# Two chunks of one image mixed in a later stage, and a finish with larger pieces, in a two-layer convolution and attention kernel

## The chip, the cores and the metric

The kernel runs on one core of one Trainium2 chip. The metric is device time in microseconds of one execution, as a median over runs. PE is TensorE (matmuls), DVE is VectorE, ACT is ScalarE, POOL is GpSimd, SP is SyncE, which issues most of the DMAs.

## The reference

Four images of 256 channels and 48 x 48 pixels go through two layers, each on a group-normalized input and each added to its input. Layer 0 is a 3 x 3 convolution and attention with 8 heads over the 2304 pixels. Layer 1 is a set of dynamic filters, mixed and normalized over all images:

```python
def _L1_conv_ref(x, W_cat, W_scale, gamma, beta):
    guidance = _conv(x, W_cat, pad=1)                  # 45 = 5 x 9 maps
    outs = [x]
    for i, d in enumerate((1, 6, 12, 24, 36)):
        w = softmax(guidance[:, 9 * i:9 * (i + 1)], axis=1)
        outs.append(_dyn_branch(x, w, d))              # 9 shifted copies, each times its map
    y = _conv(concatenate(outs, axis=1), W_scale, pad=0)   # 1536 -> 256 channels
    mean = jnp.mean(y, axis=(0, 2, 3)); var = jnp.var(y, axis=(0, 2, 3))
    return (y - mean) * rsqrt(var + EPS) * gamma + beta

x = x + _L0_conv_ref(_gn(x), ...)
x = x + _L1_conv_ref(_gn(x), ...)
```

## The kernel before, in words

The program is a fixed sequence: each engine executes its own list in order, and a list is in the order in which the Python code emits it. Semaphores join the lists. Channels lie on 128 partitions, in two halves (NH = 2). An image's rows are dealt to six chunks (NCK = 6) of 384 pixels (CH).

A loop over b runs through stages. Stage b holds the convolution and the q, k, v products of image b (`conv_qkv`: `pc` at L891, `pq` at L924, `pv` at L945) and, between their matmuls, the dynamic filters of image b-1; then attention of image b and its projection with group statistics follow. In a last stage (b == B, `alone`) image 3's filters run without a convolution beside them; then `finish` normalizes all four images and stores the result.

The filters of one image, chunk by chunk:

- guidance: `pg` (L1190) by matmuls over 45 rows in three pairs of chunks, transposed (`pt`), a softmax (`e`), transposed back (`pw`, L1244); the weights go to memory, `w_d` (L1251).
- near (dilation 1): SP loads each weight map spread over the partitions (`ws`, L1418), ACT copies it into a bank (`wb`, L1440), DVE multiplies it by the shifted image (`prod`, L1453), POOL adds it (`near`, L1458). `WBS` buffers hold loaded maps: 4, and 6 in the last stage.
- far (dilations 6 to 36): pixels are regrouped by transposes (`own`, `xa`, `xb`, L1307); weights come back by `wq` loads (L1279) and transposes `wT` (L1337) into masks (`bmat`, `amat`); matmuls (`far`, L1387) give results in banks, which `moved` (L1163 on ACT, L1165 on DVE) copies to one buffer `cat4`.
- mixes: 24 matmuls per chunk into `py` (L1536): the image itself (`gn`), four far sets, near. The result `y` is copied (L1493), its statistics are taken (L1499), and it is stored to `y_d`; image 3's stay on chip (`homes`).

`drive` decides at build time which of the streams (loads, far, near, filters, mixes) emits next. An account, `Clock`, adds up durations written in the code; a step yields the time at which it is due, and is emitted when PE's account has reached it; the convolution (`other`) fills the rest. In the last stage there is no `other`.

In the last stage `back()` loads y of images 0 and 1 and the residuals x1 of images 0, 1 and 2 (five loads of 2.36 MB on SP's queue, L1850 and L1851) when chunk 1's mixes begin; `last_loads` (from L1553) loads x1 of image 3 and y of image 2. Two groups of dummy matmuls `warm` (L970) stand at the stage's start. `finish` (from L1683) does, for images 0 and 1, 16 scalings of 576 elements on ACT and 16 sums on DVE, with one store each; for images 2 and 3, 24 scalings of 384, 12 sums of 768 and 8 stores.

Of the kernel before, what the change touches and what calls it, by code (L numbers as in the profile page):

```python
# [36 lines left out]
NEVER = float("inf")  # L37

# [17 lines left out]
def conv_preact_kernel(  # L56
# [36 lines left out]
    def rstd_of(dst, var):  # L93
        nc.vector.tensor_scalar(dst, var, EPS, None, ALU.add)
        nc.scalar.activation(dst, dst, AF.Sqrt)
        nc.vector.reciprocal(dst, dst)
# [443 lines left out]

    with tc.tile_pool(name="w", bufs=1) as wpool, tc.tile_pool(
# [93 lines left out]
        class Norm:  # L635
# [11 lines left out]
            def finish(self, psum_tile):  # L647

                mean = small.tile([P, NH], F32, tag=f"gmean{self.tag}", name=f"gmean_{self.name}", bufs=1)
                rstd = small.tile([P, NH], F32, tag=f"grstd{self.tag}", name=f"grstd_{self.name}", bufs=1)  # L650
                d2 = small.tile([P, NH], F32, tag="gd2", name=f"gd2_{self.name}")
                mv = self.mv
                for h in range(NH):
                    nc.vector.bn_aggr(mv[:, h, :], self.st[:, h].rearrange("p c s -> p (c s)"))
                yield
                pm = psum_tile(f"pm_{self.name}")
                nc.tensor.matmul(pm[:, :NH], gmat, mv[:, :, 0], start=True, stop=True)
                nc.scalar.copy(mean, pm[:, :NH])
                for h in range(NH):
                    nc.scalar.activation(  # L660
                        d2[:, h : h + 1], mv[:, h, 0:1], AF.Square, bias=mean[:, h : h + 1],
                        scale=-1.0,
                    )
                yield

                pv = psum_tile(f"pv_{self.name}")
                nc.tensor.matmul(pv[:, :NH], gmat, mv[:, :, 1], start=True, stop=False)
                nc.tensor.matmul(pv[:, :NH], gmat, d2, start=False, stop=True)
                rstd_of(rstd, pv[:, :NH])
                self.mean, self.rstd = mean, rstd  # L670
# [438 lines left out]
        def project(b, c, ao, pp, norm):  # L1109

            t = pads[b % 2]
            for o in range(NH):
                for g in range(NH):
                    nc.tensor.matmul(
                        pp[:, o, :CH],
                        wp[:, g, o * P : (o + 1) * P],
                        ao[:, g, c * CH : (c + 1) * CH],
                        start=(g == 0),
                        stop=(g == NH - 1),
                    )  # L1120
            for o in range(NH):
                x1 = inside(t, o, c * R, R)
                nc.vector.scalar_tensor_tensor(
                    out=x1, in0=rows_of(pp[:, o, :CH]), scalar=pbias[:, o : o + 1], in1=x1,
                    op0=ALU.add, op1=ALU.add,
                )
                norm.part(o, c, x1)
                nc.sync.dma_start(
                    out=rows_of(x1_d[b, :, o, c * CH : (c + 1) * CH]), in_=x1
                )  # L1130

        def dynamic_filters(b, ao, chunk, norm, other, pools):
# [27 lines left out]
            def moved(dst, src, size, *after):  # L1160

                if clock.t["ACT"] <= clock.t["DVE"]:
                    nc.scalar.copy(dst, src)  # L1163
                    return clock("ACT", 190 + 0.84 * size, *after)
                nc.vector.tensor_copy(dst, src)  # L1165
                return clock("DVE", 160 + 1.05 * size, *after)
# [12 lines left out]
            def weights(cs):  # L1179
# [61 lines left out]
                yield clock("DVE", 430) + 150  # L1241
# [44 lines left out]
            def far():  # L1286

                for c in range(NCK):
                    xT = work1.tile([P, PAIRS, C], F32, tag="xT", name=f"xT_{b}_{c}", bufs=1)

                    yield lambda: clock.t["DVE"] - 600
# [4 lines left out]
                    for h in range(NH):  # L1296
# [5 lines left out]
                            CH,  # L1302
                        )
# [38 lines left out]
                    end = clock("PE", 400)  # L1342
# [3 lines left out]
                    for t in range(3):  # L1346
# [7 lines left out]
                        end = clock("DVE", 460, end)  # L1354
                    free["k"].append(end)
                    rowsof = bmat.rearrange("p a (n y) x -> p (a n) y x", y=3)
                    for t in range(3):
                        yield lambda: clock.t["DVE"] - 600
# [9 lines left out]
                        end = clock("DVE", 960)  # L1368
                    cat = None
                    for p in range(PAIRS):  # L1370
# [25 lines left out]
                        clock("PE", 950)  # L1396
                        for s in range(2):
# [5 lines left out]
                                clock.t["PE"],  # L1403
# [7 lines left out]
            WBS, PRODS = 4 + 2 * alone, 2 + alone  # L1411
# [11 lines left out]
            def near():  # L1423

                for number, (c, k) in enumerate(sent):
                    centre = k == 4
                    if centre:
# [8 lines left out]
                        fetched[c, k][1], slot("wb", banks_w), clock.t["DVE"] - 600,  # L1436
# [71 lines left out]
            def mixes():  # L1508

                order = (0, *range(2, 2 + NF), 1)  # L1510
                for c in range(NCK):
                    now[0] = c
                    if alone and c == 1:
                        back()
                    for n in order:
# [34 lines left out]

            def last_loads():

                yield lambda: (  # L1553
                    0.0 if (NCK - 1, "own") in mixed and NCK - 1 in near_done
                    and len(far_ready) == NCK and (NCK - 2, "near") in mixed else NEVER
                )
                for o in range(NH):
                    nc.sync.dma_start(out=x1_3[:, o], in_=x1_d[B - 1, :, o])
                table(AF.Sqrt)
                for c in range(PRODS):  # L1560
                    t = work1.tile([P, NH, CH], F32, tag="prod", name=f"yp_{c}", bufs=PRODS)
                    y_2.append(t)
                    nc.sync.dma_start(out=t, in_=chunk_of(y_d, 2, c))
                yield lambda: 0.0 if (NCK - 1, "far") in mixed else NEVER
                t = work1.tile([P, NH, NF, CH], F32, tag="cat4", name="yc", bufs=1)
                t = t.rearrange("p h n c -> p (h n c)")
                for c in range(PRODS, NCK):
                    y_2.append(unit(t[:, NH * CH * (c - PRODS) : NH * CH * (c + 1 - PRODS)]))
                    nc.sync.dma_start(out=y_2[c], in_=chunk_of(y_d, 2, c))

            def drive(streams):

                due = [next(s, None) for s in streams]
                while any(d is not None for d in due):
# [9 lines left out]
                    else:  # L1584
                        got = next(other, None)
                        if got is None:
                            assert soonest < NEVER
                            clock.t["PE"] = soonest
                        else:
                            spent[0] += got  # L1590

            def warm(n):
                if alone:
                    busy(misc(f"warm_{b}_{n}"), n)
# [6 lines left out]
            warm(4)  # L1601
# [4 lines left out]
            warm(3)  # L1606
# [76 lines left out]
        def finish(work1):  # L1683

            ysc, ysh = batch_norm_of(yst, small, "f", ymv)

# [3 lines left out]
            def scaled(y, o):  # L1690
                nc.scalar.activation(
                    y, y, AF.Identity, bias=ysh[:, o : o + 1], scale=ysc[:, o : o + 1]
                )

            PART = 2 * STEP * WW
            for b, ty, tx in ((0, y_0, x1_0), (1, y_1, x1_1)):
                for o in range(NH):
                    for part in range(SIDE // 2):
                        y = ty[:, o].rearrange("p (c j w) -> p c j w", c=NCK, w=WW)
                        y = y[:, :, 2 * part : 2 * part + 2]  # L1700
                        scaled(y, o)
                        x1 = tx[:, o, part * PART : (part + 1) * PART]
                        both = x1.rearrange("p (j c w) -> p j c w", j=2, c=NCK)
                        nc.vector.tensor_tensor(
                            both, y.rearrange("p c j w -> p j c w"), both, ALU.add
                        )
                        nc.sync.dma_start(
                            out=image(b, o)[:, part * PART : (part + 1) * PART], in_=x1
                        )
            for b, ty, tx in ((2, y_2, x1_2), (3, homes, x1_3)):  # L1710
                for c in range(NCK):
                    for o in range(NH):
                        scaled(ty[c][:, o], o)
                    x1 = tx.rearrange("p h (j c w) -> p h j c w", c=NCK, w=WW)[:, :, :, c]
                    nc.vector.tensor_tensor(  # L1715
                        x1, ty[c].rearrange("p h (j w) -> p h j w", w=WW), x1, ALU.add
                    )
                for o in range(NH):
                    for cols in (slice(0, N // 2), slice(N // 2, N)):
                        nc.sync.dma_start(out=image(b, o)[:, cols], in_=tx[:, o, cols])  # L1720

        u_next = None
        norms = {}
        for b in range(B + 1):

            with tc.tile_pool(name=f"work1_{b}", bufs=2) as work1, tc.tile_pool(
                name=f"ps_c_{b}", bufs=2, space=PSUM
            ) as ps_c, tc.tile_pool(
                name=f"ps_w_{b}", bufs=2 if b == B else 1, space=PSUM
# [93 lines left out]
                else:  # L1823
                    if b == B:

                        y_0, x1_0, x1_2 = keep("q", "y_0"), keep("k", "x1_0"), keep("h", "x1_2")
                        y_1 = act.tile([P, NH, N], F32, tag="v", name="y_1")
                        x1_1, x1_3 = (t.rearrange("p h r w -> p h (r w)")[:, :, :N] for t in pads)

# [4 lines left out]
                        homes = []  # L1834
# [6 lines left out]
                        y_2 = []  # L1841
# [4 lines left out]
                        def back():  # L1846

                            for bb, ty, tx in ((0, y_0, x1_0), (1, y_1, x1_1), (2, None, x1_2)):
                                if ty is not None:
                                    nc.sync.dma_start(out=ty, in_=y_d[bb])  # L1850
                                nc.sync.dma_start(out=tx, in_=x1_d[bb])  # L1851
# [5 lines left out]
                    if b == B:  # L1857
                        finish(work1)
# [10 lines left out]
            load_pad(b)  # L1869
            scratch = upool.tile([P, NH, 3, C], F32, tag="u", name=f"scratch_{b}")  # L1870
# [100 lines left out]
```

## Time and profile before

| | us |
|---|---|
| median of 5 runs | 2794.53 (2792.67 to 2795.58) |
| profiled execution | 2793.88 |
| its span | 2792.0 |
| image 1 mixed, image 2's convolution | 1195 to 1492 |
| attention of image 2 | 1492 to 1868 |
| image 2 mixed, image 3's convolution | 1868 to 2163 |
| attention of image 3 | 2163 to 2534 |
| last stage: image 3's filters | 2534 to 2757 |
| finish | 2757 to 2792 |

The stages are cut at full microseconds: the first activation of the finish begins at 2753.75. In lines of the timeline the first number is the start in microseconds from the start of the span, the second the length, and a bracket at the end gives the idle time before it and what released it. In lines of windows each engine has its busy time and instruction count; PEclk is the granted TensorE clock, 1.00 being full.

### The profile page before, as it was taken

The numbers are of one execution on the slowest core, as the hardware profiler recorded it, in microseconds if no ns is written. First come the engines' busy times: TensorE is split into PE (matmuls) and PEld (weight loads), VectorE is DVE, ScalarE is ACT, GpSimd is POOL, SyncE is SP. The second block draws the span as 40 slices with busy tenths as digits, with TensorE's granted clock in tenths as the row PEclk, the third lists the DMA queues.
The fourth block names the chain that finished last, engine by engine and source line by source line (L and its number), as shares of the span: only waits on it lengthen the run. The fifth ranks groups of instructions, "written<-read, shape, count | busy, mean of one in ns | idle before, by whom it ended". The sixth has DMA issues, their size and how long they took to land. (4 is left out here: it accounts for less than half of the span.)

```text
span 2792.0 us, 42246 instructions
## 1 busy us (share of the span) xinstructions
PE 2651.8 (95%) x17122; PEld 1141.9 (41%) x17122; DVE 2023.7 (72%) x1948; ACT 1771.5 (63%) x2175; POOL 631.6 (23%) x583
## 2 busy tenths in 40 slices
PE   7999999899999999989999999989999999998983
PEld 5632223455652222445564222245566222234451
DVE  6578889566549888946646898875663989885665
ACT  3488988534359888833437898872334988873335
POOL 5100010535400110055510100134550000000452
PEclk9999999999999999999999999999999999999996
DMA  5514544232412544413350444522331244541545
GB/s 218 151 29 97 108 107 97 54 90 76 117 39 69 108 101 99 96 47 90 93 112 1 110 100 97 114 69 56 95 90 37 47 101 97 108 102 44 210 97 210
DMA packets 135946, 264.21 MB, mean 95 GB/s; under 512 B 65224, under 2 KB 100208, under 8 KB 134336
## 3 DMA queue, kind: packets, MB, share of 16 engines
q0 software_dynamic: 25952, 135.74, 21.1%
q1 hardware_dynamic: 109792, 125.70, 16.6%
q8 instruction: 136, 2.23, 0.3%
q14 instruction: 66, 0.54, 0.1%
HBM read 105.82 MB, written 32.89 MB: 50 GB/s over the span
## 5 line engine op out<-in xcount | busy, mean ns | idle before, releaser
L1044 DVE TENSOR_TENSOR acc<-acc,p 128x2048 f32<-128x2048 f32 (+1 forms) x572 | 1061.2, 1855 | 113.1 <-ACT p L1008 61.9
L1008 ACT ACTIVATE p<-se 128x1536 f32<-128x1536 f32 x648 | 938.6, 1448 | 0.0
L999 PE MATMUL so<-q,k 32*128 32x512 f32 (+1 forms) x1440 | 726.4, 592 | 14.1 <-ACT p L1007 13.6
L999 PE MATMUL se<-q,k 32*128 32x512 f32 (+1 forms) x4320 | 735.0, 592 | 0.0
L1028 PE MATMUL num<-p,vT 128*32 128x512 f32 (+1 forms) x5760 | 703.5, 560 | 4.6 <-ACT p L1008 2.4
L1007 ACT ACTIVATE p<-so 128x512 f32<-128x512 f32 x648 | 388.4, 599 | 184.1 <-PE se L999 74.7
L1458 POOL TENSOR_TENSOR near<-near,prod 128x768 f32<-128x768 f32 x192 | 348.2, 1814 | 401.3 <-DVE prod L1453 392.1
L999 PEld LDWEIGHTS so<-q,k 32*128 32x128 f32 x1440 | 216.1, 183 | 529.2 <-ACT p L1007 490.1
L1028 PEld LDWEIGHTS num<-p,vT 128*32 128x32 f32 x5760 | 132.9, 108 | 478.1 <-issue 444.3
L1048 POOL DMA_DIRECT2D scratch<-p x124 | 105.5, 851 | 770.2 <-ACT p L1008 566.0
L1536 PE MATMUL py<-far,wsc 128*128 128x384 f32 x768 | 256.8, 489 | 0.0
L1453 DVE TENSOR_TENSOR prod<-wb,pad 128x768 f32<-128x768 f32 x192 | 182.3, 955 | 99.1 <-ACT wb L1440 58.6
L1440 ACT COPY wb<-ws 128x384 f32<-128x384 f32 x216 | 107.9, 501 | 210.1 <-DVE prod L1453 194.9
L999 PEld LDWEIGHTS se<-q,k 32*128 32x128 f32 x4320 | 226.7, 183 | 5.4 <-ACT p L1008 4.1
L1536 PEld LDWEIGHTS py<-far,wsc 128*128 128x128 f32 x768 | 144.8, 191 | 100.1 <-issue 5.2
L1046 POOL DMA_DIRECT2D scratch<-p x32 | 17.9, 559 | 696.0 <-ACT p L1008 485.6
L1163 ACT COPY far<-far 128x512 f32<-128x512 f32 x82 | 87.9, 1099 | 127.2 <-PE far L1387 127.2
L891 PE MATMUL pc<-cv_q,u 128*128 128x288 f32 x576 | 155.1, 417 | 8.9 <-DVE cv_q L782 6.4
L1190 PE MATMUL pg<-pad,wcat 128*45 128x384 f32 x864 | 152.0, 497 | 6.5 <-DVE pad L631 4.0
L891 PE MATMUL pc<-cv_k,u 128*128 128x288 f32 x576 | 152.7, 410 | 1.6 <-ACT m L837 1.3
L891 PEld LDWEIGHTS pc<-cv_q,u 128*128 128x128 f32 x576 | 108.3, 193 | 47.2 <-DVE cv_q L782 6.5
L924 PE MATMUL pq<-hid,wqkv 128*128 128x384 f32 x384 | 125.3, 487 | 1.1 <-ACT q L931 0.6
(246 smaller groups left out, 2350.3 us busy)
## 6 DMA issues: line engine op xcount, KB each, us to landing
scratch<-p POOLq DMA_DIRECT2D x156, 768.0 KB, 5.7
ws<-w_d SPq DMA_DIRECT2D x216, 192.0 KB
pad<-in_x SPq DMA_DIRECT2D x14, 1152.0 KB
u<-u_d SPq DMA_DIRECT2D x18, 768.0 KB
x_d<-pad SPq DMA_DIRECT2D x48, 192.0 KB
xst<-in_x POOLq DMA_DIRECT2D x36, 192.0 KB, 6.2
y_d<-y SPq DMA_DIRECT2D x15, 384.0 KB
u_d<-u SPq DMA_DIRECT2D x6, 768.0 KB
```

The lines of the kernel that those rows point to most:

```text
L891: nc.tensor.matmul(m, u[:, h, kx, o * P : (o + 1) * P], halves[g][:, h, i, :, kx : kx + WW], start=(h == 0 and kx == 0), stop=(h == NH - 1 ...
L924: nc.tensor.matmul(pq[:, :CH], wqkv[:, i, s, g * P : (g + 1) * P], hid[:, i, cols], start=(i == 0), stop=(i == NH - 1),)
L999: nc.tensor.matmul(dst[:, at : at + n], k_[r, g, m * P : (m + 1) * P], q[r, g, q0 : q0 + n], start=True, stop=True,)
L1007: nc.scalar.activation(p[:, 0, :], s1, AF.Exp, scale=QS)
L1008: nc.scalar.activation(p[:, 1:, :], s3, AF.Exp, scale=QS)
L1028: nc.tensor.matmul(st["num"][r, at : at + n], vT[:, m, g * P + j * D : g * P + (j + 1) * D], p[:, j, at : at + n], start=(m == 0 and not s ...
L1044: nc.vector.tensor_tensor(st["acc"][:, js], other[:, js], p[:, js], ALU.add)
L1190: nc.tensor.matmul(pg[64 * s : 64 * s + NG, :CH], wcat[:, ii, k, :], shifted(ii, cc, k // 3 - 1, k % 3 - 1), start=(i == 0 and k == 0), st ...
L1440: nc.scalar.copy(pw[:, :CH], fetched[c, k][0])
L1453: nc.vector.tensor_tensor(prod.rearrange("p h (r w) -> p h r w", w=WW), wb, src, ALU.mult)
L1458: nc.gpsimd.tensor_tensor(cat, cat, prod, ALU.add)
L1536: nc.tensor.matmul(py[c][:, o, :CH], wsc[:, n * NH + i, o * P : (o + 1) * P], rhs, start=(n == 0 and i == 0), stop=(n == order[-1] and i = ...
```

## The change

- Chunks 5 and 4 of image 2 (`LATE`) are not mixed in the stage of image 2. When their near and far results are there, SP stores image rows, near and far results to `late_d`. Chunk 5's are loaded again before attention of image 3, chunk 4's at the start of the last stage. `late()` mixes both there, as `other`, which the planner puts wherever no stream is due. Image 3's own mixes wait until it is over. The two `warm` groups in that stage go.
- In the last stage three `ws` buffers are kept instead of six, and `back()` is called at chunk 2's mixes instead of chunk 1's.
- x1 of image 3 is neither stored nor loaded: the finish takes it from the normalized image as gn x std + mean.
- `finish` takes the images in the order 0, 2, 3, 1. Images 0 and 1: ACT scales 1152 elements at a time, DVE adds in pieces of 576 or 1152. Images 2 and 3: ACT adds the shift to the residual (1152 at a time), and DVE does scale and sum in one instruction of 384.
- In the planner near and far steps may be emitted 2500 ns of account ahead of DVE instead of 600; the far stream's first yield is 0; several durations are larger.

The diff, cut to its core:

```diff
+LATE = (5, 4)
+AHEAD = 2500.0
...
+    late_d = tc.dram_tile([len(LATE), P, NH * (2 + NF), CH], F32, name="late_d")
...
-                yield clock("DVE", 430) + 150
+                yield clock("DVE", 1100 if pair else 320) + 150
...
-                    yield lambda: clock.t["DVE"] - 600
+                    yield 0.0
...
-                        yield lambda: clock.t["DVE"] - 600
+                        yield lambda: clock.t["DVE"] - AHEAD
...
-            WBS, PRODS = 4 + 2 * alone, 2 + alone
+            WBS, PRODS = 4 - alone, 2 + alone
...
-                        fetched[c, k][1], slot("wb", banks_w), clock.t["DVE"] - 600,
+                        fetched[c, k][1], slot("wb", banks_w), clock.t["DVE"] - AHEAD,
...
-                    if alone and c == 1:
+                    if alone and c == 0:
+                        yield lambda: 0.0 if over[0] else NEVER
+                    if alone and c == 2:
                         back()
+                    if b == B - 2 and c in LATE:
+                        yield lambda: max(
+                            t[c][1] if c in t else NEVER for t in (near_done, far_done)
+                        )
+                        to = late_d[LATE.index(c)]
+                        for h in range(NH):
+                            nc.sync.dma_start(
+                                out=rows_of(to[:, h]), in_=gn[:, h, lines(c), 1 : 1 + WW]
+                            )
+                        nc.sync.dma_start(out=to[:, NH : 2 * NH], in_=near_done[c][0])
+                        nc.sync.dma_start(
+                            out=to[:, 2 * NH :],
+                            in_=far_done[c][0].rearrange("p h n c -> p (h n) c"),
+                        )
...
+                        continue
...
+            def late():
+                for j, c in enumerate(LATE):
+                    t = lates[j]
...
+                    for o in range(NH):
+                        for n in range(2 + NF):
+                            for i in range(NH):
...
+                                nc.tensor.matmul(both[:, o, :CH], ..., t[:, at], ...)
+                                clock("PE", MM)
+                                if n <= NF or i < NH - 1:
+                                    yield MM
+                        nc.scalar.copy(y[:, o], both[:, o, :CH])
...
+                        nc.vector.bn_stats(yst[:, o, (B - 2) * NCK + c, :], y[:, o])
+                        yield MM
+                over[0] = True
...
+            if alone:
+                other = late()
...
-            warm(4)
...
-            warm(3)
...
+            def far_end(b, ty, tx, of, bias, scale):
                 for o in range(NH):
+                    for r in (0, HH // 2):
+                        nc.scalar.activation(
+                            rows_of(tx[:, o])[:, r : r + HH // 2], of(o, r), AF.Identity,
+                            bias=bias[:, o : o + 1],
+                            scale=1.0 if scale is None else scale[:, o : o + 1],
+                        )
...
+                    for c in range(NCK):
...
+                        nc.vector.scalar_tensor_tensor(
+                            out=x1, in0=rows_of(ty[c][:, o]), scalar=ysc[:, o : o + 1], in1=x1,
+                            op0=ALU.mult, op1=ALU.add,
+                        )
...
+            near_end(0, y_0, kept["x1_0"])
+            far_end(
+                2, y_2, x1_2, lambda o, r: rows_of(x1_2[:, o])[:, r : r + HH // 2], ysh, None
+            )
+            far_end(
+                3, homes, y_0, lambda o, r: inside(pads[(B - 1) % 2], o, r, HH // 2), both,
+                norm.std,
+            )
+            near_end(1, kept["y_1"], kept["x1_1"])
...
+                        nc.sync.dma_start(out=lates[1], in_=late_d[1])
```

## The prediction

> **What bounds the kernel now.** I read the page's engine totals first, then busy time by stage, then what PE waits for in the two stages that the change touches, then the last microseconds of the timeline.
>
> ```profile
> PE 2651.8 (95%) x17122; PEld 1141.9 (41%) x17122; DVE 2023.7 (72%) x1948; ACT 1771.5 (63%) x2175; POOL 631.6 (23%) x583
> ```
>
> PE is the bound on average. The stages say where it is not (columns: window, length, then busy PE, PEld, DVE, ACT, POOL, granted clock, DMA share, GB/s):
>
> ```profile
> 1868.00:2163.00 295.00, 288.29 (x1265) 177.15 (x1264) 155.12 (x230) 104.08 (x177) 120.32 (x72) 1.00 0.27 70
> 2534.00:2757.00 223.00, 190.56 (x830) 102.41 (x826) 127.60 (x184) 72.05 (x119) 88.36 (x51) 0.93 0.42 129
> 2757.00:2792.00 35.00, 0.00 (x0) 0.00 (x0) 21.27 (x25) 23.36 (x36) 0.00 (x0) 0.50 0.67 263
> ```
>
> The first row is image 2's mixing beside image 3's convolution: PE is busy for all but 6.7 us. The second is the last stage, image 3's filters with no convolution beside them: 32 us idle, clock 0.93. The third is the finish without PE. In the last stage PE's idle time is many short waits (waited for, total, times, longest):
>
> ```profile
> PE pw L1244 <- DVE e L1240: 4.9, 3, 3.1
> PE far L1387 <- ACT far L1163: 4.5, 6, 0.8
> PE wT L1337 <- DMA wq<-w_d: 2.7, 2, 2.4
> PE py L1536 <- ACT yu L1493: 2.7, 3, 0.9
> ```
>
> So the change moves PE work from a full stage into one with holes.
>
> **Part 1, the mixes taken from image 2's stage.** Two chunks are 2 x 24 matmuls of 2 instructions each, 96 in all. A row with 96 of the same shape:
>
> ```profile
> 2114.25 31.12 PE L924 MATMUL pq<-hid,wqkv 128*128 128x384 f32 x96
> ```
>
> 31.1 us go, nearly all of it time of the path, since PE is full there. What comes: SP stores each late chunk's operands (near, four far, two strided pieces of gn, 2.36 MB) to memory. The far operands sit in one buffer (cat4). The next chunk's far copies on ACT may not write it until the store has read it, and SP issues chunk 4's store only after weight load ws_2_5_3, which waits for a copy on ACT just ahead of the far copies. Behind those copies on ACT and on the two far banks stand PE's next far matmuls. Store: 2.3 us issue, 2.3 for gn in 192-byte pieces, 1.0 for near and 3.9 for far by size at 0.4 MB/us, all estimates from the page's rates, near 9.6, plus 2.2 for two copies of 1.1 = 11.8 us; convolution matmuls queued in between cover 4.4 to 5.9. I take 8 of stall and 1.7 of half clock behind it. Sum -31.1 + 8 + 1.7 = **-21.4** (-31 if the store is covered, -14 if it is twice as slow). The other DVE work of the late chunks (2 x 0.8 of yu copies, statistics) was beside PE.
>
> **Part 2, loads asked for earlier and new durations.** The planner may issue near and far steps 2500 instead of 600 ns ahead of DVE, in the stages of images 0 and 1 too. Walking the order on PE, some guidance waits (pg for a bank, about 1.8 us) come and pw waits (about 1.8) go. No row prices the rest. A gain is bounded by these stages' idle time, 6.7 us each (297.00 - 290.31 for image 1's); a loss by products (0.955 us each, L1453) that now stand ahead of a copy which PE awaits, say in 8 of the 12 chunks. I take **0**, which the balanced walk is nearest to, and -4 to +8.
>
> **Part 3, the last stage.** PE's own work after the projection (end 2539.7), by rows: six mixes 288 x 0.324 = 93.3; guidance 3 x 11.94 = 35.8; far 18 x 1.07 = 19.2; transposes xa, xb 6 x 0.8 and wT 6 x 0.85 = 9.9; small ones 3: 161.2 in all. PE now ends at 2751.0, 211.3 later: 4.7 are warming matmuls, 45 are waits and slow clock. With the late 31.1 in place of the warming the work is 192.3. Then the waits that I find by walking the new order on the engines: late's second bank of y 1.8; pad 1.5; the flag pf, whose DVE input now queues behind products, 3.9; wT, whose load stands behind ws_3_0_8 on SP, 3.0; small ones and the last copy 5.2. The loads of the late chunks (2.36 MB, some 6 us at 0.4 MB/us, the second needed some 40 us after its issue), their 4 copies on ACT and 4 statistics on DVE are hidden: ACT is busy for 72 of 223 us and DVE for 128; if that cover failed, each would cost about 0.6 at a bank of y.
>
> The largest is new. The five loads back (11.8 MB) move from chunk 1's mixes to chunk 2's, and the weight buffers (ws) from six to three. Before:
>
> ```profile
> 2622.14 0.42 SPq L1850 DMA_DIRECT2D y<-y_d  x1
> 2624.47 0.86 SPq L1851 DMA_DIRECT2D x<-x_d  x1
> 2629.96 3.10 SPq L1279 DMA_DIRECT2D wq<-w_d  x4
> 2653.92 0.90 PE L1337 MATMUL wT<-ident,wq 36*64 36x36 f32 x12 [2.38 <-DMA wq<-w_d]
> 2656.39 0.48 ACT L1440 COPY wb<-ws 128x384 f32<-128x384 f32 x1 [4.45 <-DVE bmat L1347]
> 2658.93 0.48 ACT L1440 COPY wb<-ws 128x384 f32<-128x384 f32 x1 [2.06 <-DMA ws<-w_d]
> ```
>
> A small load (wq) issued 7.8 us behind them landed only at about 2653.9: 11.8 MB hold the queue for 31.8 us. Then six buffered copies bridged it, and PE lost 2.4. After: SP passes the loads at about 2667.5 (behind ws_3_3_0), the next ws lands near 2698.5. ACT has three copies in hand; the fourth stops at the head of its queue, and far_3_3_0's copy stands behind it and two more, until about 2702.6. PE reaches far_3_3_1 at about 2685.5: 17.1 us of stall, 1.7 of half clock. PE's end: 2539.7 + 192.3 + 1.8 + 1.5 + 3.9 + 3.0 + 5.2 + 17.1 + 1.7 = 2766.2, **+15.2** (-12 with no such waits but the small ones, +26 at a slower drain). POOL, last on the path now by 2.0 us, needs 21 more adds of 1.81 = 38 after 2702.6, until 2741, and is covered.
>
> **A rule weighed.** The removed warming is dear by these two rows:
>
> ```profile
> 2539.51 1.89 PE L970 MATMUL warm<-wsc,ident 128*128 128x256 f32 x8
> 2544.46 2.79 PE L970 MATMUL warm<-wsc,ident 128*128 128x256 f32 x6 [0.25 <-DVE grstd_n L94]
> ```
>
> 0.24 us each against 0.47: after short waits PE runs at half speed, in stretches whose clock records are 3.41 or 6.83 us. I charge half a record of 3.4 us, 1.7, to each long stall. The Trainium skill, "TensorE: Matmul & The Clock Gate", Part 1, says that the default is throttled: one idle window of about 3.4 us halves the clock and a busy one restores it. By it a stall of 17 us costs a whole slow window, an estimate of 1.7 us as I have it, but the short holes should cost nothing, which the second row contradicts; by the rule alone the late matmuls win nothing from the clock.
>
> **Part 4, the finish.** Before, shift ready at 2753.7 to the end 2792.0: 38.3 us. ACT was serial throughout, and the last four stores came late:
>
> ```profile
> 2753.75 12.24 ACT L1691 ACTIVATE y<-y,ysh_f,ysc_f 128x576 f32<-128x576 f32 x16 [0.82 <-DVE ysh_f L170]
> 2780.39 0.96 DVE L1715 TENSOR_TENSOR pad<-wqkv,pad 128x768 f32<-128x768 f32 x1 [0.24 <-ACTq L1899]
> 2781.38 3.01 SPq L1720 DMA_DIRECT2D out<-pad  x4
> ```
>
> After: ACT 16 of 1152 elements, 1.25 each by the slope of 576 (0.765) and 384 (0.61): 20 us. DVE: 8 sums of 0.76 and 4 of 1.36, 11.5, and 24 fused of 384 at 0.56, 13.4 (by the slope of 576 and 768); with the start behind ACT 27.6 us to the last sum, then a last store of 0.6 to 1.2 MB at 0.4 MB/us and its latency: 32.7. **-5.6** (-8 to -3; 9.44 MB at 0.4 MB/us alone need 24). The 12 stores of x1 that leave attention 3, and the load of 2.36 MB that leaves the last stage, were hidden: 0.
>
> **Sum.** 2792.0 - 21.4 + 0 + 15.2 - 5.6 = 2780.2 of span; 1.9 around it (2793.88 - 2792.0) gives 2782.1, and the median stands 0.65 above the profiled execution: **2782.5**.
>
> **Rivals.** (a) Neither load nor store blocks: ws loads slip between, or the copies have gone ahead. Last stage 18.8 less: 2763.7; without the store's wait too, 2754. For it: the stall rests on the order of three ACT copies. Against: the queue rows above. (b) Slower: the holes of the last stage don't go. They are latencies inside filter chains, and late's matmuls stand mostly before far of chunk 1, while 45 us of waits and slow clock lie throughout. If all 45 stay, not the 15.4 that I count beside the 18.8, PE ends 29.6 later: 2812. It decides from 17.6 us of the 29.6, at 2800.1. Against: pf, pw and the early dips are where late goes. (c) No change: the moved steps cost 4 us, four products of 0.955, in each of three convolution stages through DVE's queue: 2794.5. The conv rows show few waits, but nothing there bounds a moved product.
>
> **Chances.** What a measurement of this kernel can tell from no change is 0.2%, 5.6 us: faster is below 2788.9, slower above 2800.1. Forecast 0.45 (own range 2771 to 2792; faster 0.39, same 0.06), (a) 0.22, (b) 0.20 (slower 0.18, same 0.02), (c) 0.13 (faster 0.01, same 0.09, slower 0.03). Faster 0.62, same 0.17, slower 0.21. The range 2760 to 2803 leaves out part of (a) below and half of (b) above.
>
> **What would show it.** Image 2's stage near 274 us with a far matmul waiting some 8 us for ACT; PE waiting 15 to 20 us at far of chunk 3 in the last stage, ACT waiting there for ws; finish near 33 us. No wait over 5 us at far of chunk 3 means (a); last-stage PE idle over 50 us in many short waits means (b); longer stages of images 0 and 1 mean (c).

## The result, and the profile after

Time after: 2796.6 us median of 24 runs (2793.99 to 2801.52); ratio to the kernel before 1.0009, 95% interval 1.0003 to 1.0014. The forecast was 2782.5 and faster by 0.4%: no gain came. The profiled execution has a span of 2793.9 us, 1.9 more than before.

The stages, cut at the same PE instructions in both profiles (the first matmul of the statistics after a projection, `pm_n`, and `pb`, the first after the convolution's products), so that a stage can be compared although it starts earlier or later:

| stage | before, us | after, us | difference | forecast |
|---|---|---|---|---|
| to the first attention | 146.4 | 147.8 | +1.4 | 0 |
| attention 0 | 384.2 | 384.6 | +0.4 | 0 |
| image 0 mixed | 286.7 | 285.7 | -0.9 | 0 (this and the next two of its kind: part 2) |
| attention 1 | 384.3 | 387.9 | +3.6 | 0 |
| image 1 mixed | 286.7 | 285.7 | -1.1 | 0 |
| attention 2 | 385.7 | 384.8 | -0.9 | 0 |
| image 2 mixed | 286.7 | 268.8 | -17.9 | -21.4 |
| attention 3 | 381.9 | 382.2 | +0.3 | 0 |
| last stage, to PE's end | 208.4 | 228.9 | +20.6 | +15.2 |
| PE's end to the end | 41.0 | 37.5 | -3.5 | -5.6 |
| span | 2792.0 | 2793.9 | +1.9 | -11.8 |

Busy time in image 2's mixing, the last stage and the finish from the shift on, in the windows of the changed kernel (columns as in the windows of before):

```profile
1876.53:2145.31 268.78, 253.80 (x1140) 157.02 (x1138) 152.70 (x219) 99.58 (x171) 114.78 (x68) 0.98 0.35 98
2527.48:2756.41 228.93, 201.93 (x881) 108.83 (x879) 120.55 (x162) 70.23 (x118) 87.06 (x48) 0.95 0.35 109
2760.01:2793.90 33.89, 0.00 (x0) 0.00 (x0) 23.38 (x37) 19.56 (x16) 0.00 (x0) 0.52 0.71 280
```

PE's idle time in image 2's stage is 15.0 us (5.4 before, in the same cut), and in the last stage 27.0. What PE waits for in the changed kernel, the two longest in image 2's mixing that are new, then the two longest in the last stage (waited for, total, times, longest):

```profile
PE far L1395 <- ACT far L1170: 7.0, 1, 7.0
PE pc L897 <- DVE yt L832: 1.8, 1, 1.8
...
PE far L1395 <- ACT far L1170: 17.4, 1, 17.4
PE pf L1723 <- DVE okay L1720: 3.5, 1, 3.5
```

The many short waits of before (pw 4.9, far 4.5, yu 2.7) are gone, and two long single ones stand in their place. The first, in the timeline of SP, ACT and PE:

```profile
2059.83 12.43 SPq L1426 DMA_DIRECT2D ws<-w_d  x3
2075.13 0.40 SPq L1535 DMA_DIRECT2D late_d<-far  x1
2071.44 0.47 ACT L1448 COPY wb<-ws 128x384 f32<-128x384 f32 x1
2081.76 1.95 ACT L1170 COPY far<-far 128x512 f32<-128x512 f32 x2 [9.85 <-DMA late_d<-far]
2082.86 2.97 PE L1395 MATMUL far<-amat,xT 64*128 64x256 f32 x8 [7.00 <-ACT far L1170]
```

SP gets past the third ws load only when ACT's copy at 2071.44 has freed a buffer; then come image rows, near, and at 2075.13 the far store. ACT, next in its list, stands for 9.85 us until the store has read the buffer, and PE behind it for 7.0.

The second, in the last stage (PE, then SP, then ACT):

```profile
2673.01 0.70 PE L1395 MATMUL far<-amat,xT 64*128 64x256 f32 x2
2691.13 2.07 PE L1395 MATMUL far<-amat,xT 64*128 64x256 f32 x6 [17.42 <-ACT far L1170]
2693.13 2.93 PE L1562 MATMUL py<-near,wsc 128*128 128x384 f32 x4
...
2655.08 0.42 SPq L1927 DMA_DIRECT2D y<-y_d  x1
2657.41 0.72 SPq L1927 DMA_DIRECT2D pad<-x_d  x1
2658.86 0.81 SPq L1426 DMA_DIRECT2D ws<-w_d  x2
...
2660.80 0.49 ACT L1448 COPY wb<-ws 128x384 f32<-128x384 f32 x1
2687.99 1.01 ACT L1448 COPY wb<-ws 128x384 f32<-128x384 f32 x2 [26.71 <-DMA ws<-w_d]
2689.99 1.09 ACT L1170 COPY far<-far 128x512 f32<-128x512 f32 x1
```

The five loads are issued from 2655.08 to 2658.1. The weights issued right behind them are there only at 2688: ACT idles for 26.71 us with three buffers used up, and the far copy that PE needs is behind the weight copies in ACT's list. In the row after the wait four matmul instructions of py take 2.93 us, where four of the same kind take 1.56 in the chunk before: the clock is halved (the last section has the windows).

### The profile page after: what moved, and what is told of

Its sections match the earlier page's. It is cut to its first block, busy times and chain, and to the rows that moved or that the text cites. A ratio compares the mean times of both kernels' runs of the same rounds, so it can differ in the third digit from the quotient of the medians.

```text
span 2793.9 us, 42183 instructions
## 1 busy us (share of the span) xinstructions
PE 2644.1 (95%) x17108; PEld 1139.0 (41%) x17108; DVE 2024.9 (72%) x1955; ACT 1762.3 (63%) x2154; POOL 632.1 (23%) x583
## 3 DMA queue, kind: packets, MB, share of 16 engines
q0 software_dynamic: 25952, 135.74, 21.4%
## 5 line engine op out<-in xcount | busy, mean ns | idle before, releaser
L1005 PE MATMUL so<-q,k 32*128 32x512 f32 (+1 forms) x1440 | 726.4, 592 | 13.0 <-ACT p L1013 11.8
L1562 PE MATMUL py<-far,wsc 128*128 128x384 f32 x704 | 236.7, 488 | 0.0
L1052 POOL DMA_DIRECT2D scratch<-p x32 | 17.9, 559 | 670.8 <-ACT p L1014 524.0
L1562 PEld LDWEIGHTS py<-far,wsc 128*128 128x128 f32 x704 | 131.1, 190 | 87.3 <-issue 1.8
```

What stands on the lines that cost most here:

```text
L1005: nc.tensor.matmul(dst[:, at : at + n], k_[r, g, m * P : (m + 1) * P], q[r, g, q0 : q0 + n], start=True, stop=True,)
L1562: nc.tensor.matmul(py[c][:, o, :CH], wsc[:, n * NH + i, o * P : (o + 1) * P], rhs, start=(n == 0 and i == 0), stop=(n == order[-1] and i = ...
```

## The experiments

The theory: the mixing that was moved is worth something, and two waits that came with it, both of DMAs standing in front of small ones, take it back. The rivals are written in each expectation. Ratios are to the kernel before, with 95% intervals; 0.1% is 2.8 us.

**Far store early.**

```diff
-                        yield lambda: max(... near_done, far_done)
-                        (stores: image rows, near, far)
+                        yield lambda: far_done[c][1] if c in far_done else NEVER
+                        (store: far)
+                        yield lambda: near_done[c][1] if c in near_done else NEVER
+                        (stores: image rows, near)
```

> Edit: in the changed kernel the far results of a late chunk are stored as soon as they are there, ahead of its near results and image rows. Theory (the store of chunk 4's far results, issued behind a weight load that waits for ACT, holds the far copies of chunk 5): PE's 7.0 us wait at far in image 2's stage and the half clock behind it go, that stage gets 9 to 10 us shorter, the time 7 to 11 us less than the changed kernel's. Rival (the convolution's own evictions bound that stretch, and the wait only stands in front of them): another wait takes its place, under 3 us gained.

2788.74 us, ratio 0.9978 (0.9969 to 0.9987). Image 2's stage is 260.1 us instead of 268.8, no far wait is left in it, and nothing else took its place. The theory holds: some 9 us by the ratios and by the stage, where 9 to 10 were expected of the stage.

**Loads back, spread.**

```diff
-                    if alone and c == 2:
-                        back()          # five loads
+                    if alone and c < 5:
+                        back(c)         # one load
```

> Edit: in the changed kernel the five loads back are issued one at a time, at the start of the mixes of chunks 0 to 4, instead of together at chunk 2. Theory (11.8 MB in one piece hold the queue for some 26 us, longer than three weight buffers last): PE's 17.4 us wait at far of chunk 3 and the half clock behind it go, the last stage gets 18 to 21 us shorter, the time 17 to 21 us less than the changed kernel's. Rival 1 (each single load holds the weights for some 6 us, too): five waits of 2 to 4 us in its place, at most 8 us gained. Rival 2 (POOL's sums of near are the real bound of the last stage): PE waits for POOL at the near matmuls instead, at most 8 us gained.

2780.73 us, 0.9951 (0.9938 to 0.9964). The last stage goes from 228.9 to 210.4 us. PE's longest waits there now:

```profile
PE pf L1723 <- DVE okay L1720: 3.5, 1, 3.5
PE wT L1345 <- DMA wq<-w_d: 2.4, 1, 2.4
```

The 17.4 us are gone whole, and PE waits for no far copy and for no sum of POOL: both rivals fall. The stage is 18.5 us shorter, as expected; the time fell by 16, a little less than the 17 to 21 expected.

**Both.**

> Both edits: early far store and spread loads. Theory: the two gains add, 26 to 31 us less than the changed kernel's, some 2767, and faster than the kernel before by 24 to 29 us. Rival (the mixing moved only shifts work between stages that are bound in the end by the same chain): the sum is less than 12 us.

2767.26 us, 0.9903 (0.9889 to 0.9918): image 2's stage 258.4, last stage 209.3. Against the changed kernel that is 29 us, within what was expected. Alone, the edits gave some 9 and 16 us by the ratios; the 4 us between that sum and 29 are within the intervals. With the two waits gone the change does what it says.

**The planner's part alone**, on the kernel before.

> The kernel before with nothing but the planner's new durations and the 2500 ns of lead. Theory (the account moves steps but no work; the 3.6 us by which attention 1 is longer in the changed kernel's profile is from execution to execution): within 2 us of the kernel before. Rival (the account costs): 3 to 6 us more, in attention 1 again.

2807.97 us, 1.0046 (1.0033 to 1.0059). The theory fell: the planner's part costs 12.7 us, and not in attention 1 (385.4) but in the last stage, 219.1 instead of 208.4. Its PE waits and DVE's timeline:

```profile
PE pw L1245 <- DVE e L1241: 23.8, 2, 23.1
...
2635.87 0.44 DVE L1232 TENSOR_TENSOR e<-pt,mx 128x270 f32<-128x270 f32 x1
2661.27 0.96 DVE L1448 TENSOR_TENSOR near<-wb,pad 128x768 f32<-128x768 f32 x1 [24.96 <-ACT wb L1442]
```

With 2500 ns of lead, near products come ahead of the last part of a softmax in DVE's list. Their weights stand behind the loads back (still at chunk 1's mixes), so DVE idles for 24.96 us and PE waits 23.1 us for the softmax. It is the same DMA queue, met by another engine. The lead and the durations were changed together here, and no run parts them.

**No late chunk.** LATE is empty; the rest as in the changed kernel.

> The changed kernel with no chunk of image 2 mixed late (all six in image 2's stage, nothing stored for later, the warming still gone; loads back, three weight buffers, planner and finish as changed). Theory (late's matmuls fill holes of the last stage, and the 17 us stall at the loads back stays): image 2's stage 17 us longer than the changed kernel's, the last stage 5 to 11 us shorter, some 2803 to 2810. Rival (the last stage does not hide late's 31 us): last stage 31 us shorter, some 2783.

2799.39 us, 1.0012 (1.0003 to 1.0022), between theory and rival: image 2's stage is 285.7 (+16.9 against the changed kernel), the last stage 213.5 (-15.4). PE's longest wait for a far copy is 11.6 us there, where the theory left it at 17. As the change was made, mixing two chunks late brings nothing that can be measured: 1.0009 with it and 1.0012 without.

**The finish alone**, with the last residual from the normalized image: the changed kernel with all its other parts undone.

> The new finish and the last residual from the normalized image alone: no late chunk, warming, six weight buffers, loads back at chunk 1 and the old planner as before. Theory: the finish is 3.5 to 5.6 us shorter and nothing else moves, 2789 to 2791. Rival (the removed stores and loads of the last residual also shorten the last stage): 2784 to 2788.

2797.07 us, 1.0008 (0.9999 to 1.0017). The stretch from PE's end on is 37.4 us instead of 41.0, so the finish itself is 3.6 us shorter; the time shows none of it, and the interval leaves no room for it. In this profile attention 1 is 1.7 and the first stage 1.8 us longer. Neither theory nor rival holds for the time.

**Loads back on POOL's queue.**

```diff
-                                nc.sync.dma_start(out=kept[name], in_=src)
+                                nc.gpsimd.dma_start(out=kept[name], in_=src)
```

> The changed kernel with its five loads back issued by POOL, on POOL's own queue, at the same point (chunk 2). Theory (the weights stand behind 11.8 MB in the order of SP's one queue): with a queue of their own the loads no longer stand ahead of the weights, PE's 17.4 us wait shrinks to under 6, and the time by 11 to 20. Rival (the DMA engines' rate is what lacks, whatever the queue): the wait stays over 12 us, the time within 6 of the changed kernel's.

2798.9 us, 1.0011 (1.0002 to 1.002), and PE's far wait is 17.4 us again. ACT's copies of the weights in that stretch, after one at 2663.02:

```profile
2672.55 0.48 ACT L1448 COPY wb<-ws 128x384 f32<-128x384 f32 x1 [9.04 <-DMA ws<-w_d]
2678.54 0.48 ACT L1448 COPY wb<-ws 128x384 f32<-128x384 f32 x1 [5.50 <-DMA ws<-w_d]
2691.82 0.48 ACT L1448 COPY wb<-ws 128x384 f32<-128x384 f32 x1 [12.79 <-DMA ws<-w_d]
```

On one queue nothing passed; on two, a weight load comes through every 6 to 13 us. The trace's packets show how: in the 4 us from 2677.6 on, in which the engines move 439 GB/s, there are 88 packets of 18,432 bytes from POOL's queue and 88 of 1,536 bytes from SP's, and from 2665 to 2686 there are 425 and 418: one for one. A weight load has 128 of the small packets, 8 on each of 16 engines. If each waits for one large packet of 0.69 us (the median in the trace), that is an estimate of 8 x 0.69 = 5.5 us for what alone would take under 1 (192 KB at 0.4 MB/us); it fits the shortest of the intervals, not the longest. "DMA: Bandwidth & Descriptors" of the Trainium skill, section "Queues, rings and completion order", says that an engine goes round the queues with work by whole packets; the equal counts of this run agree. The rival's forecast held, and its reason in part: in windows of 4 us from 2661 to 2689 the DMA share is 0.93 to 1.08, so the engines were full; which of the loads waited went by packets, not by bytes.

**Both, with the old planner.**

> Early far store and spread loads (2767 us) with the planner's old durations and 600 ns of lead. Theory (once nothing long stands in the queue, the lead is worth little: mixes of images 0 to 2 were 1 us shorter each with it): 2768 to 2774. Rival (with the old lead image 1's attention loses the 3 us that it is longer in all runs of the changed kernel): 2762 to 2766.

2785.78 us, 0.9961 (0.9948 to 0.9974): 16 us more than with the new planner by the ratios, neither theory nor rival. Attention 3 takes 400.0 us instead of 382.1. What PE waits for in attention 3, and POOL's sums of near around its start (2135.5):

```profile
PE se L1005 <- DVE prod L1461: 7.8, 1, 7.8
...
2127.52 1.81 POOL L1466 TENSOR_TENSOR near<-near,prod 128x768 f32<-128x768 f32 x1 [42.05 <-DVE prod L1461]
```

POOL stood idle for 42 us because chunk 5's near products came late under the old planner; the convolution's stage, 29 us shorter than before, ran out, and the products ended in attention 3, ahead of its own work on DVE. Without the new planner late mixing keeps little of its worth: 0.9961 here, against 0.998 for the kernel before with its loads spread and no late chunk (below).

**No late chunk, loads spread.**

> No late chunk and the loads back spread over the mixes of chunks 0 to 4; the rest as in the changed kernel. Beside the run with both edits (2767) it prices the late mixing itself without the two waits. Theory (the last stage hides about half of late's 31 us): image 2's stage 286, last stage some 198 to 200, in all 2782 to 2786. Rival 1 (the holes go by the new lead alone, not by late's matmuls; late costs its full 31 us there): last stage 178 to 185, in all 2763 to 2770. Rival 2 (late is hidden whole): last stage 207 to 210, in all 2791 to 2795.

2782.7 us, 0.9960 (0.9945 to 0.9976), within the theory's range, though the last stage is 1.5 us shorter than it said: image 2's stage 285.8, last stage 196.5. Against the run with both edits, late mixing takes 27.4 us from the one and adds 12.7 to the other: 0.57% or 16 us in the time, some half of the 31 us moved.

**One late chunk.**

> Early far store and spread loads, but only chunk 5 of image 2 mixed late, and five weight buffers (the second late result's room). Theory (each chunk takes 15 us from image 2's stage and adds less to the last): between the run with both (2767) and the run without late, some 2773 to 2778. Rival (the second chunk only costs): 2760 to 2766.

2773.88 us, 0.9923 (0.9908 to 0.9938): some 10 us better than none and 6 worse than two. Image 2's stage 273.9, last stage 200.1.

**Table loaded early**, with both edits.

> Early far store and spread loads, and ACT's table for the last square root loaded at chunk 5's mixes instead of after the last copy. Theory (the table load of 1.28 us stands on the path between the last statistics and the finish): 0.9 to 1.3 us less than with both, 2765 to 2767, and the fastest kernel of all. Rival (DVE's chain there is as long): no change.

2767.01 us, 0.9898 (0.9882 to 0.9915). The stretch after PE's end is 0.8 us shorter (36.7); the time cannot be told from the run with both. It is the fastest kernel here by a hair, 1.0% faster than before.

**Spread loads alone, and with the planner's part**, on the kernel before.

> The kernel before with its five loads back spread over the mixes of chunks 0 to 4, and nothing else. Theory (with six weight buffers and the old lead the loads cost the kernel before only the 2.4 us of one wait and little beside): 2 to 4 us less than the kernel before. Rival (the loads alone were worth the 13 us by which the run without late chunks gained from spreading them): 9 to 13 us less.

> The kernel before with the new durations and lead, and the loads back spread. Theory (the lead puts products ahead of the softmax on DVE, and cost 12.7 us only because their weights stood behind the loads): the 23.1 us wait of pw goes, last stage 195 to 200 us, 7 to 11 us less than the kernel before, attention 1 at 385 to 386. Rival (the lead itself costs): the time at or above the kernel before's.

2791.16 us, 0.998 (0.9971 to 0.9989), and 2780.01 us, 0.9944 (0.9928 to 0.996). Spreading alone is worth 0.2% or some 5.5 us, more than the theory and less than the rival said; last stage 205.5. With it the lead that cost 12.7 us gains 10: last stage 194.1, the wait for pw down to 1.7 in all, and 16 us less than the kernel before where 7 to 11 were expected. So 16 of the 27 us that the run with both edits gains on the kernel before come without any late mixing. Attention 1 is 384.1 and 384.8 in the two.

## Why the prediction was wrong

The mechanism was right, and both new waits were found and sized: at the far store 8 us forecast and 7.0 measured, at the loads back 17.1 and 17.4, pf 3.9 and 3.5, wT 3.0 and 2.3. Rival (a), no such waits, was priced well as a difference: 18.8 us for the loads' wait (2763.7) and 9.7 more for the store's (2754); removing the first gave 16 (2780.73), removing both 29 (2767.26). What failed is the sum, in two terms above all: PE's own work in the last stage, 192.3 us in part 3 and 201 measured, and the slow clock behind a long wait, 1.7 us each and 2.7 and 3.4 measured. Forecast gains of 36.7 us stood against 24.9 of costs, and 13.7 us, nearly all on one side, were missing. (The last line of the sum also adds up to 2782.7, not 2782.5.)

- **Part 3, the last stage, +22.9 for +15.2.** The forecast counts from the projection's end (the cut at pm_n gives 2.3 us of late's matmuls to attention 3). From there PE needed 234.2 us where 226.5 were forecast, and 211.3 before (before, then after):

```profile
2539.70:2751.00 211.30, 185.26 (x808) 98.77 (x806) 120.62 (x168) 68.12 (x112) 86.98 (x48) 0.94 0.42 129
2522.24:2756.41 234.17, 205.24 (x891) 110.84 (x890) 123.20 (x168) 70.23 (x118) 87.06 (x48) 0.95 0.35 106
```

  Idle time was less than forecast, 28.9 against 32.5. The slow clock was more: half a record (1.7) was charged once, and it cost 2.7 behind the long wait (far, py and far take 6.13 us where such matmuls take some 3.4) and about 1.6 behind pf, which was charged nothing. The rest, 8.7 us, is PE's work: I priced every matmul of a mix by a run of 96 in a row, 0.324 us; in the changed kernel's timeline four near instructions between two far sets take 1.49 us, 0.373 each, and a chunk's round of mix, far and transposes takes 20.96 us where my rows give 20.4. Taking every matmul from its start to the next one's, without idle time and corrected to full clock, the six mixes need 96.8 us (93.3 forecast), the late chunks 33.1 (31.1), guidance 37.0 (35.8) and the small ones 4.1 (3); far and the transposes are within 0.6 us.

  The profile of before shows the same. In its row PE is idle for 26.0 us, and a mean clock of 0.94 over 211.3 us costs at most 12.7 more. The prediction put 45 us on waits and slow clock, so at least 6 of these were PE's own work, which no moved matmul can fill.
- **Part 1, image 2's stage, -17.9 for -21.4.** The wait was 1 us shorter; the slow clock behind it 3.4 us, not 1.7 (eight far instructions 2.90 instead of 1.06 from start to start, sixteen of pc 5.51 instead of 3.99); and a wait of 1.8 us for the convolution's own DVE step (yt), which the profile of before does not have, was not foreseen.
- **Part 4, the finish, -3.5 for -5.6.** From the shift on it took 33.9 us, not 32.7, and a load of ACT's table got onto the path ahead of the square root:

```profile
2757.60 1.28 ACT L611 ACT_TABLE_LOAD   x1
2780.55 5.30 DVE L1752 TENSOR_TENSOR pad<-y,pad 128x1152 f32<-128x1152 f32 x6
2781.93 6.80 SPq L1755 DMA_DIRECT2D out<-pad  x6
```

  The last sums are still followed by stores that end 5 us after their issue. And the time showed nothing of it: the finish alone measured 1.0008.
- **The stages priced at nothing, +2.8 for 0,** or +0.5 without the 2.3 us in attention 3. The mixes of images 0 and 1 each gained 1 us by the planner. Attention 1 lost 3.6. It takes 384.1 to 385.4 us in the four profiles of kernels built on the one before, and 386.0 to 388.3 in the eleven of kernels built on the changed one, whose attention code is the same; attention 0, from 384.2 to 387.4 in these profiles, shows no such split. No run isolates this, and its cause stays open, as does the place where the finish's 3.6 us go.

Part 2 was right in its two stages and missed where the planner acts most: in the last stage it costs 12.7 us or gains 10, depending on what stands in the DMA queue, and it carries the near products of image 2 through the shortened stage (18 us). Rival (b) had the direction of part 3 right, but not the holes that it named: those went. That the time fell where rival (c) put it is luck: the convolution stages, where (c) looked for the loss, lost nothing to the planner.

The range to 2803 held the time; the forecast's place in it did not, because each small unknown was taken at its middle or at nothing, and nearly all came out dearer. No run shows one common cause for them.

## What to carry to other kernels

Before moving work, list the large DMAs and the small ones that the critical engines need behind them: 11.8 MB in one piece cost 16 to 20 us here with three buffers and some 5.5 in the kernel before with six (no run changes the buffers alone), and in five pieces PE waited for none of it. Before counting the rest of a stage as holes, take its idle time and its clock from one row of windows. Price a long wait of PE with its slow clock, some 3 us more, and matmuls in short mixed groups by such groups. What an account's lead and durations are worth hangs on what stands in the queues; test them together, since the same edit cost 13 us and gained 10.

## What the runs showed of the hardware

After both long waits of the changed kernel the granted clock stayed at half well after PE was busy again (columns as before; the 7 us wait, then the long one):

```profile
2082.05:2085.47 3.42, 2.61 (x8) 1.67 (x8) 0.36 (x1) 2.95 (x5) 0.00 (x0) 0.50 0.00 0
2085.47:2088.88 3.41, 3.41 (x8) 2.26 (x8) 3.38 (x4) 1.59 (x2) 1.89 (x1) 0.50 0.33 58
2088.88:2092.29 3.41, 3.41 (x17) 2.47 (x17) 2.08 (x5) 1.41 (x3) 0.00 (x0) 1.00 0.00 0
2689.62:2693.04 3.42, 1.91 (x6) 1.17 (x6) 3.42 (x4) 2.58 (x4) 3.28 (x2) 0.50 0.81 165
2693.04:2696.45 3.41, 3.41 (x7) 1.64 (x8) 2.00 (x3) 1.18 (x3) 3.25 (x3) 0.50 0.37 116
2696.45:2699.86 3.41, 3.41 (x16) 2.03 (x15) 2.52 (x3) 2.94 (x4) 2.55 (x2) 1.00 0.01 5
```

PE started again at 2691.13 and had its full clock at 2696.45, 5.3 us later; behind the 7 us wait it had it at 2088.88, 6.0 us after 2082.86. The two stretches of half clock, 20.48 and 10.24 us, are whole multiples of 3.41 us, and the rows are cut by that step. "TensorE: Matmul & The Clock Gate" of the Trainium skill, Part 1, says that one busy window of about 3.4 us releases the throttle; in the rows the full clock follows the first step that PE fills, and the partly filled one ahead of it (1.91 and 2.61 us busy) adds to the time. So half clock after such a wait lasts one to two steps, 3.4 to 6.8 us, and costs half of that, 1.7 to 3.4: an estimate from these lengths, in which the measured 2.7 and 3.4 lie.

A step need not be idle to lose the clock. In the kernel before, one in which PE was busy for 1.99 of 3.41 us was followed by one at half clock, which bears out what the prediction took from its second row of warm:

```profile
2674.35:2677.76 3.41, 1.99 (x22) 1.42 (x19) 3.03 (x5) 2.72 (x4) 0.80 (x1) 1.00 0.40 84
2677.76:2681.17 3.41, 3.41 (x9) 1.88 (x8) 2.65 (x5) 0.00 (x0) 1.81 (x1) 0.50 0.29 59
```

A second queue did not protect small loads from large ones: with packets of 18,432 and 1,536 bytes served in equal numbers, a load of 192 KB came through every 6 to 13 us instead of none in 27, and the kernel was no faster.
